# Entering the step loop of a graph kernel while the last sums before it still run

## The chip, the cores and the metric

The kernel runs on one core of a Trainium2 chip. The metric is the device time of one execution in microseconds (us): 748.04 us is the median of three runs of the kernel before (744.8 to 749.22). The engines are named as in the profile: PE is the matrix engine and PEld its weight load, DVE the vector engine, ACT the scalar engine, POOL the GpSimd engine. SP only issues transfers; ACT and POOL issue some too. Each engine works through its instructions in the order in which they were put on it, and an instruction that waits holds up those behind it.

## What is computed

Four graph layers over 2708 nodes with 128 features each; the adjacency `adj` is a 0/1 matrix. Each layer adds its result to x after a layer norm and a relu. The change lies in the last layer:

```
XW = X @ W                                  # 2708 x 128
s_col = XW @ a[:128];  s_row = XW @ a[128:]
den = exp(leaky_relu(s_row[:, None] + s_col[None, :], slope=0.01))
num = A @ den                               # 2708 x 2708, A is adj
att = where(num != 0, den / num, 0)
H   = A @ (att @ XW)
```

## The kernel before

The kernel doesn't compute num as a full matrix product. It ranks the nodes by s_row and cuts the ranking into chunks of `CH` = 124 nodes. For a column of den the leaky relu is on one branch for all nodes below a certain rank and on the other for all above it, so of num only the one chunk in which the branch changes needs a product over single nodes; all the others enter as prefix sums over whole chunks. The columns are put into 22 tables of 128 (`NE`), two chunks each, so there are 44 "slots" (`NS`).

The stage before the loop makes what the loop reads:

- `sums` (L1249): PE multiplies chunk weights `wts` with the transposed adjacency `adjt8`, kept in SBUF as fp8, 22 row tiles by 6 column blocks of 450 or 452 (`BLK`), into six PSUM accumulators. Row tiles 0 to 15 come for all blocks; the last `NTAIL` = 6 row tiles come pair by pair: blocks (0,3), (1,4), (2,5).
- For each pair (L1447 to L1470): DVE and ACT copy the accumulators to `s_sb`, PE turns them into prefix sums (L1456), ACT copies those to `flat` (L1462), DVE splits them into a high and a low half (`pre_hi` L1463, `pre_lo` L1464), and SP and ACT store these to `pre_d` in DRAM (L1468): 88 rows of 2708, four rows for each chunk.
- The table product (L1481): from `lanes_j` and `rhs_j` PE makes the table `jt`, from which DVE takes `c_two` (L1485 to L1492) and the indices `xw_i`. `c_two` is turned (L1501) and stored to `ctwo_d` (L1504).
- `first_densities` (L1550): DVE makes a diagonal of the first four slots' `c_two`, PE spreads it over all partitions with a product with `ones` (L1559), ACT makes the exponentials of both branches (`exponents`, L1530 and L1533), DVE their maximum and its two halves `d_hi`, `d_lo` (`densities`, L1542 to L1546).

What a slot q needs besides its densities is a tile `r` of 128 x 2708: rows 0 to 123 are adjacency rows, gathered by POOL as one byte each (`fetch`, L1512) and widened by DVE (`widen`, L1592, 124 x 2708); rows 124 to 127 are the four prefix rows of its chunk, loaded by SP from `pre_d` (`fetch_pre`, L1584), at an address that SP first reads from `pre_i` (`value_load`, L1583). Six tiles `r` and six `g` rotate.

The loop (L1630 on) has 22 steps s. Step s takes slots 2s and 2s+1 and makes, for each of six column blocks (`E0`, five of 512 and one of 148), four matmuls (L1646) and a logarithm on ACT (L1647); ACT then inverts (`invert`, L1619), DVE weighs (`weigh`, L1625), and two steps later PE adds the values into six accumulators (`spread_value`, L1600). Beside that each step makes the densities of two slots four ahead: SP loads their `c_two` values, spread over 128 partitions, from `ctwo_d` (`fetch_c`, L1570, 128 KB), and ACT makes the four exponentials after blocks 1 and 2. Every even step ACT issues a load of 1354 KB of the adjacency (`fetch_check`, L699), and every odd step DVE checks it (L695). After the last step the values go through one more product over all rows (after `lp.close()`); its rows come partly from tiles loaded during the last steps (`soon`, L1676).

The order on an engine comes from a planner, which lists instructions by the order in the text and by when it thinks their inputs are ready. Where `in_order()` or `pin` stands, an instruction is bound behind what was traced before it on its engine. In the kernel before, the stretch from L1438 to L1504 is left to the planner; the loop's matmuls, ACT and DVE work, gathers and row loads are pinned, `fetch_c` and `value_load` are not.

## Time and profile before

| what | us |
|---|---|
| median of three runs | 748.04 |
| the profiled execution, its own time | 749.01 |
| its span, first to last instruction | 747.1 |
| PE busy in the span | 656.5 (88%) |
| DVE busy | 583.3 (78%) |
| ACT busy | 468.7 (63%) |
| loop matmuls (L1646): first and last start | 450.1 and 664.8 |
| mean granted PE clock | 0.951 |

Positions in the profile are microseconds from the first instruction. The span is 1.9 us shorter than the profiled execution's own time, and that execution took 1.0 us more than the median. A row of the timeline gives start, duration, engine, line, operation, the tiles written and read, the shape and the count; in square brackets stands how long the engine had been idle before and what ended that. A row of busy time by stretch gives, for each engine, the busy time and in parentheses the number of instructions, and then the granted PE clock (1.00 is full speed), the mean busy share of the 16 DMA engines, and GB/s.

### The profile page before, as it was taken

Reading aid. Unit: us, or ns where it says so; the run is one execution under the profiler, and the core shown is the slowest. Engines: PE = TensorE matmul, PEld = TensorE weight load, DVE = VectorE, ACT = ScalarE, POOL = GpSimd, SP = SyncE. Lnnn points to the kernel's source line nnn. Section 1 sums busy time; section 2 is a strip of 40 time slices with the busy share of each in tenths; the row PEclk is TensorE's granted clock in tenths of the full one; section 3 lists DMA queues with packets and bytes.
Section 4 is the critical chain, followed back from the end, with each engine's and each line's share of the span. In section 5 each row is a group of like instructions: output and inputs, shape, how many; then the busy total and the mean of one; then the engine's idle time right before and its main releaser. Section 6 shows DMA issues by size and latency. Waiting matters only on the chain.

```text
span 747.1 us, 8635 instructions
## 1 busy us (share of the span) xinstructions
PE 656.5 (88%) x2775; PEld 421.5 (56%) x2775; DVE 583.3 (78%) x1019; ACT 468.7 (63%) x694; POOL 221.7 (30%) x198
## 2 busy tenths in 40 slices
PE   6889888978999999866998946999999999999994
PEld 3433333425678677634455614566666666657783
DVE  5999967968867885753798853999899899748972
ACT  5766667748856654425574533888888888765452
POOL 3320000141200210014570524366766766100000
PEclk9999998999999999986998986999999999999997
DMA  9699999765650799400100239857786776658711
GB/s 332 255 376 422 425 428 394 277 261 209 269 186 3 241 303 360 159 0 15 43 22 2 62 116 125 205 143 166 183 177 152 191 159 151 156 197 328 254 34 52
DMA packets 48679, 146.29 MB, mean 196 GB/s; under 512 B 12546, under 2 KB 27390, under 8 KB 40198
## 3 DMA queue, kind: packets, MB, share of 16 engines
q1 hardware_dynamic: 29288, 87.00, 34.6%
q10 hardware_dynamic: 4714, 34.74, 13.4%
...
## 4 chain that ended last, share of the span: by engine, by line
PE 50%; issue 15%; DVE 12%; ACT 7%; DMA 6%; POOL 3%; SPq 1%; ACTq 0%; POOLq 0%; DVEq 0%
PE bank L1646 14%; PE acc L1600 13%; PE acc L1763 5%; PE acc L614 5%; PE acc L1249 4%; DVE chk L695 3%; DMA chk<-in_adj_t_dram 2%; DVE m L483 2%; DMA adj_d<-a 2%; ACT adjt L216 2%; ACT y L474 1%; DMA c_row<-ctwo_d 1%; PE acc L1114 1%; POOL rstd L157 1%; PE bank L1012 1%
## 5 line engine op out<-in xcount | busy, mean ns | idle before, releaser
L1646 PE MATMUL bank<-r,d_hi 128*128 128x512 f32 (+1 forms) x264 | 142.3, 543 | 15.4 <-DMA r<-pre_d 9.7
L1600 PE MATMUL acc<-e,xw 128*128 128x512 f32 (+1 forms) x264 | 120.6, 544 | 0.0
L1647 ACT ACTIVATE ln<-bank,tiny 128x512 f32<-128x512 f32 x132 | 84.0, 636 | 48.7 <-PE bank L1646 43.2
L340 PE MATMUL acc<-tau,hw 128*128 128x512 f32 (+1 forms) x240 | 101.7, 572 | 12.9 <-DVE tau L348 12.9
L1512 POOL DMA_INDIRECT g<-adjt_d,row_i x44 | 90.5, 2057 | 37.5 <-DVE r L1592 14.3
L1646 PE MATMUL bank<-r,d_lo 128*128 128x512 f32 (+1 forms) x264 | 99.8, 382 | 0.0
L481 ACT CAST m<-a 128x660 fp32r<-128x660 fp8e4 (+1 forms) x45 | 55.2, 1233 | 53.1 <-PE acc L1763 30.7
L340 PEld LDWEIGHTS acc<-tau,hw 128*128 128x128 f32 x240 | 44.5, 197 | 71.9 <-issue 46.1
L1625 DVE SCALAR_TENSOR_TENSOR e<-row_b,sig,ln 128x1536 f32<-128x1536 f32 (+3 forms) x46 | 71.4, 1559 | 14.2 <-PE bank L1646 11.2
L348 DVE SCALAR_TENSOR_TENSOR tau<-row_b,sg,a 128x1536 f32<-128x1536 f32 (+1 forms) x44 | 70.8, 1623 | 11.1 <-DMA a<-in_adj_dram 10.1
L1646 PEld LDWEIGHTS bank<-r,d_hi 128*128 128x128 f32 x264 | 51.5, 195 | 48.9 <-issue 29.2
L695 DVE SCALAR_TENSOR_TENSOR chk<-chk 128x2708 f32<-128x2708 f32 (+1 forms) x22 | 65.4, 2975 | 10.2 <-DMA chk<-in_adj_t_dram 10.2
L1592 DVE CAST r<-g 124x2708 fp32r<-124x2708 fp8e4 x44 | 70.4, 1643 | 0.0
L371 ACT ACTIVATE a<-a 128x2708 fp8e4<-128x2708 f32 x22 | 54.1, 2458 | 24.7 <-issue 11.8
L1646 PEld LDWEIGHTS bank<-r,d_lo 128*128 128x128 f32 x264 | 51.6, 196 | 29.4 <-issue 24.0
L1619 ACT ACTIVATE ln<-ln 128x512 f32<-128x512 f32 (+2 forms) x68 | 62.8, 926 | 0.6 <-ACT ln L1647 0.6
L157 POOL TENSOR_TENSOR rstd<-isq,neg_half 128x4 f32<-128x4 f32 (+1 forms) x24 | 28.4, 1184 | 116.6 <-DVE isq L156 77.8
L1512 POOL DMA_INDIRECT xw<-xw_d,xw_i x22 | 41.6, 1892 | 62.5 <-PE acc L1600 52.2
L483 DVE CAST m<-a 128x2048 fp32r<-128x2048 fp8e4 (+1 forms) x43 | 39.5, 920 | 20.6 <-PE acc L614 11.1
L1600 PEld LDWEIGHTS acc<-e,xw 128*128 128x128 f32 x264 | 47.8, 189 | 12.2 <-issue 3.8
L614 PE MATMUL acc<-m,y_hi 128*128 128x512 f32 (+1 forms) x132 | 49.8, 384 | 5.4 <-DVE m L600 2.0
L614 PE MATMUL acc<-m,h_hi 128*128 128x512 f32 (+1 forms) x132 | 53.9, 416 | 0.1
...
## 6 DMA issues: line engine op xcount, KB each, us to landing
...
```

Of the source, the lines that this page charges most:

```text
L340: nc.tensor.matmul(accs[b][:, : hi - lo], stationary, tau[b // 3][:, o : o + hi - lo], start=first, stop=last)
L348: nc.vector.scalar_tensor_tensor(tau, row_b[:, h0:h1], sg[:, t : t + 1], tiles_a[t][:, h0:h1], ALU.max, ALU.mult)
L481: nc.scalar.copy(m[:, : hi - lo], src[:, lo:hi])
L614: nc.tensor.matmul(sums_of[phase, b][:, : hi - lo], part[:, t, :], tiles_m[k][:, lo - base : hi - base], start=t == 0 and i == 0, stop=t = ...
L695: lambda: nc.vector.scalar_tensor_tensor(a[:r], a[:r], 1.0, a[:r], ALU.is_equal, ALU.not_equal, accum_out=odd[:r, t : t + 1])
L1512: return nc.gpsimd.indirect_dma_start(out=out, out_offset=None, in_=src, in_offset=bass.IndirectOffsetOnAxis(ap=idx, axis=0),)
L1592: ins = nc.vector.tensor_copy(rows_r[q][:CH], g[:CH])
L1600: m = nc.tensor.matmul(ys_acc[b][:, : hi - lo], xws[s], waiting[s][:, lo:hi], start=(s == 0), stop=(s == NE - 1))
L1619: pin(nc.scalar.activation(lns[s][:, lo:hi], lns[s][:, lo:hi], AF.Exp, scale=-1.0))
L1625: nc.vector.scalar_tensor_tensor(waiting[s][:, lo:hi], row_b[:, lo:hi], sig[:, s : s + 1], lns[s][:, lo:hi], ALU.max, ALU.mult)
L1646: pin(nc.tensor.matmul(num[:, : hi - lo], d, a[:, lo:hi], start=(i == 0), stop=(i == 3)))
L1647: pin(nc.scalar.activation(lns[s][:, lo:hi], num[:, : hi - lo], AF.Ln, bias=tiny))
```

## The change

Only the stretch before the loop, the first step and the places of some tiles change; the same values are computed.

- The sums use the loop's column blocks `E0` instead of `BLK`.
- Each pair of column blocks gets a DRAM table of its own, `early_d[i]`. `store_pre(i)` stores a pair's prefix rows to it (two stores from SP, two from ACT), stores them to `pre_d` as well (four from SP), and loads the rows of slots 0 and 1 from `early_d[i]` into the pair's columns of `r` (four loads from SP).
- Slots 0 and 1 are gathered and widened before the sums end, into tiles of the pool `plan`, which is free by then; the gathers of slots 2 to 5 go to the pools `slot` and `steps`, which lie where `adjt8` lay. So six `g` tiles are two in `plan` and four in `slot`, and six `r` tiles are two of three tiles `wide3` in `plan` (the third is `ln` of the even steps) and four in `steps`.
- The whole stretch stands in `in_order()`. The table product comes right after the first pair's sums, the densities of slots 0 to 3 between the pairs; PE spreads `c_two` of slots 4 to 7 too (`cp4`), so that `fetch_c` begins with slot 8.
- Each `value_load` is bound behind the SP transfer traced before it (`chunk_of`).
- Step 0 takes its column blocks in the order 0, 3, 1, 4, 2, 5.
- Four tiles instead of six are loaded ahead for the last product (`soon`).

```diff
-
-    plan = ctx.enter_context(tc.tile_pool(name="plan", bufs=1, side="right", reuse_waits="tile"))
+    early_d = [dram.tile([4 * NC, 2 * 512], F32R, name=f"early_d{i}") for i in range(3)]
+
+    plan_stack = ExitStack()
+    plan = plan_stack.enter_context(tc.tile_pool(name="plan", bufs=1, side="right", reuse_waits="tile"))
...
-        bits = tabs.tile([P, N], BF16, tag="bits", name="bits", bufs=3)
+        bits = plan.tile([P, N], BF16, tag="wide3", name="bits", bufs=3)
...
-            junk = tabs.tile([P, N], BF16, tag="junk", name="junk", bufs=1)
+            junk = tab.tile([P, N], BF16, tag="far_off", name="junk")
...
         for b in blocks:
-            lo, hi = BLK[b]
+            lo, hi = E0[b]
...
-    pairs = [(b, b + 3) for b in range(3)]
...
+    def chunk_of(q):
+        traced = nc.cur_bb.bb.instructions
+        n = len(traced)
+        chunk_before = nc.sync.value_load(pre_i[0:1, q : q + 1], min_val=0, max_val=NC - 1)
+        load = traced[n]
+        issued = next(i for i in reversed(traced[:n]) if i.engine == load.engine and "DMA" in type(i).__name__)
+        tc.add_manual_dep(
+            load,
+            issued.name,
+            mybir.DependencyInfo(mybir.DependencyClass.NoSync, mybir.DependencyReason.DATA),
+            reason="chunk_of",
+        )
+        return chunk_before
+
+    def fetch_into(q, pool):
+        g = pool.tile([P, N], U8, tag="g8", name="g8", bufs=2 if pool is plan else 4)
+        pin(gather(g[:CH], adjt8_d[:, :], row_i[:CH, q : q + 1]))
+        rows8[q] = g
+
+    def widen(q):
+        g = rows8.pop(q).bitcast(F8)
+        pin(nc.vector.tensor_copy(rows_r[q][:CH], g[:CH]))
+
+    for q in range(2):
+        fetch_into(q, plan)
+    first_chunks = [chunk_of(q) for q in range(2)]
+    for q in range(2):
+        rows_r[q] = plan.tile([P, N], F32R, tag="wide3", name="r", bufs=3)
...
-    for i, pair in enumerate(pairs):
+
+    def evacuate(i):
+        for h, b in enumerate((i, i + 3)):
+            w = E0[b][1] - E0[b][0]
+            (nc.scalar.copy if h else nc.vector.tensor_copy)(s_sb[: 6 * NW, h, :w], SUMB[b][: 6 * NW, :w])
+
+    def last_sums(i):
         for t in range(T - NTAIL, T):
-            sums(t, pair)
+            sums(t, (i, i + 3))
+
...
-        lo, hi = BLK[i]
-        w = hi - lo
-        for h in range(2):
-            nc.scalar.copy(flat[64 * h : 64 * h + 2 * NC, lo:hi], p[64 * h : 64 * h + 2 * NC, :w])
-        ts_(pre_hi[:W108, lo:hi].bitcast(I32), flat[:W108, lo:hi].bitcast(I32), -4096, None, ALU.bitwise_and)
-        nc.vector.tensor_sub(pre_lo[:W108, lo:hi], flat[:W108, lo:hi], pre_hi[:W108, lo:hi])
-        for o, part_sb in ((0, pre_hi), (2 * NC, pre_lo)):
...
+        return p
+
+    def flatten(i, p):
+        for h, b in enumerate((i, i + 3)):
...
+    def store_pre(i):
+        pair = (i, i + 3)
+        ts_(pre_hi[:W108].bitcast(I32), flat[:W108].bitcast(I32), -4096, None, ALU.bitwise_and)
+        nc.vector.tensor_sub(pre_lo[:W108], flat[:W108], pre_hi[:W108])
+        parts = [(o, h, part_sb) for o, part_sb in ((0, pre_hi), (2 * NC, pre_lo)) for h in range(2)]
+        wide = [E0[b][1] - E0[b][0] for b in pair]
+        for o, h, part_sb in parts:
+            (nc.scalar if h else nc.sync).dma_start(
+                early_d[i][o : o + 2 * NC, h * 512 : h * 512 + wide[h]].bitcast(F32),
+                part_sb[64 * h : 64 * h + 2 * NC, : wide[h]],
+            )
+        for o, h, part_sb in parts:
+            lo, hi = E0[pair[h]]
+            nc.sync.dma_start(pre_d[o : o + 2 * NC, lo:hi].bitcast(F32), part_sb[64 * h : 64 * h + 2 * NC, : wide[h]])
+        early_rows = early_d[i].rearrange("(f c) n -> f (c n)", c=NC).bitcast(F32)
+        for q in range(2):
+            for h, b in enumerate(pair):
+                lo, hi = E0[b]
+                nc.sync.dma_start(
+                    rows_r[q][CH:, lo:hi].bitcast(F32),
+                    early_rows[:, bass.ds(first_chunks[q] * 1024 + h * 512, hi - lo)],
                 )
...
-    FIRST = 4
-    p = bank()
-    nc.tensor.transpose(p[:NS, :P], c_two_f, ident)
-    ctwo_t = row("ctwo_t", P)
...
+    diag = tab.tile([P, 8, P], F32, tag="far_off", name="diag")
...
+    def diagonal(s0):
...
+    def spread_c(s0):
+        p = acc_bank(0 if s0 == 0 else 3)
+        nc.tensor.matmul(p, ones, diag[:, s0 : s0 + 4].rearrange("p s q -> p (s q)"), start=True, stop=True)
+        return p
+
+    def first_exponents(s0, p):
...
+    def first_densities(s0):
...
+    with in_order():
+        last_sums(0)
+        evacuate(0)
+        jp = bank()
+        for t in range(T):
+            nc.tensor.matmul(jp[:, : 6 * NC], lanes_j[:, t, :], rhs_j[:, t, :], start=(t == 0), stop=(t == T - 1))
+        z4 = tab.tile([P, 4, P], F32, tag="lanes", name="z4")
+        low4 = tab.tile([P, 4, P], F32, tag="rhs", name="low4")
+        widen(0)
+        p0 = prefixes(0)
+        jt = row("jt", 6 * NC)
+        nc.vector.tensor_copy(jt, jp[:, : 6 * NC])
...
+        nc.vector.tensor_sub(c_two[:, :, 0], c_tab, gone)
+        nc.vector.scalar_tensor_tensor(c_two[:, :, 0], second, -3.0e4, c_two[:, :, 0], ALU.mult, ALU.add)
+        ts_(second, second, -1.0, 3.0e4, ALU.add, ALU.mult)
+        nc.vector.tensor_add(c_two[:, :, 1], gone, second)
+        diagonal(0)
+        flatten(0, p0)
+        store_pre(0)
+        last_sums(1)
+        p = bank()
+        nc.tensor.transpose(p[:NS, :P], c_two_f, ident)
+        cp = spread_c(0)
+        evacuate(1)
+        ctwo_t = row("ctwo_t", P)
+        nc.scalar.copy(ctwo_t[:NS], p[:NS, :P])
+        nc.sync.dma_start(ctwo_d.rearrange("(s q) -> s q", q=P), ctwo_t[:NS])
...
+        p1 = prefixes(1)
+        first_exponents(0, cp)
+        first_densities(0)
+        flatten(1, p1)
+        last_sums(2)
+        store_pre(1)
+        widen(1)
+        first_exponents(2, cp)
+        evacuate(2)
+        cp4 = spread_c(4)
+        first_densities(2)
+        p2 = prefixes(2)
+        nc.scalar.activation(sig, c_tab, AF.Exp, scale=0.99)
+        flatten(2, p2)
+        store_pre(2)
...
     def density_tiles():
-        z = steps.tile([P, 2, P], F32, tag="z", name="z", bufs=3)
+        z = steps.tile([P, 2, P], F32, tag="z", name="z", bufs=2)
...
-    def first_densities():
...
-            densities(s0, z, lower)
-
-    c_rows = {}
+    c_rows = {4: cp4[:, : 2 * P], 6: cp4[:, 2 * P :]}
 
     def fetch_c(s0):
         c_rows[s0] = p = steps.tile([P, 2 * P], F32, tag="c_row", name="c_row", bufs=3)
         nc.sync.dma_start(p, ctwo_d[s0 * P : (s0 + 2) * P].partition_broadcast(P))
...
     def fetch(q):
-        g = plan.tile([P, N], U8, tag="g8", name="g8", bufs=6)
-        pin(gather(g[:CH], adjt8_d[:, :], row_i[:CH, q : q + 1]))
-        rows8[q] = g
-
-    pre_rows = pre_d.rearrange("(f c) n -> f (c n)", c=NC).bitcast(F32)
+        fetch_into(q, plan if q % 6 < 2 else slot)
 
     def fetch_pre(q):
-        r = rows_r[q] = steps.tile([P, N], F32R, tag="r", name="r", bufs=6)
-        chunk_before = nc.sync.value_load(pre_i[0:1, q : q + 1], min_val=0, max_val=NC - 1)
+        if q % 6 < 2:
+            r = plan.tile([P, N], F32R, tag="wide3", name="r", bufs=3)
+        else:
+            r = steps.tile([P, N], F32R, tag="r", name="r", bufs=4)
+        rows_r[q] = r
+        chunk_before = chunk_of(q)
         pin(nc.sync.dma_start(r[CH:, :].bitcast(F32), pre_rows[:, bass.ds(chunk_before * N, N)]))
...
-    for q in range(6):
+    for q in range(2, 6):
         fetch(q)
-    for q in range(6):
+    for q in range(2, 6):
         fetch_pre(q)
     for s in range(2):
         fetch_xw(s)
-    first_densities()
-    for q in range(2):
-        widen(q)
-    for s in range(2):
-        fetch_c(FIRST + 2 * s)
     lns, soon = {}, {}
...
     for s in range(NE):
-        coming = FIRST + 2 * s
+        coming = 4 + 2 * s
         if coming + 4 < NS:
             fetch_c(coming + 4)
-        if coming < NS:
+        fresh = coming < NS
+        if fresh:
             z, lower = density_tiles()
         if s + 2 < NE:
             fetch_xw(s + 2)
         for q in (2 * s + 2, 2 * s + 3):
             if q < NS:
                 widen(q)
-        lns[s] = steps.tile([P, N], F32, tag="ln", name="ln", bufs=2)
-        for b, (lo, hi) in enumerate(E0):
+        if s % 2:
+            lns[s] = steps.tile([P, N], F32, tag="ln", name="ln", bufs=1)
+        else:
+            lns[s] = plan.tile([P, N], F32, tag="wide3", name="ln", bufs=3)
+        for i, b in enumerate((0, 3, 1, 4, 2, 5) if s == 0 else range(NB)):
+            lo, hi = E0[b]
             num = bank()
-            for i in range(4):
-                d, a = dense[2 * s + i // 2][i % 2], rows_r[2 * s + i // 2]
-                pin(nc.tensor.matmul(num[:, : hi - lo], d, a[:, lo:hi], start=(i == 0), stop=(i == 3)))
+            for j in range(4):
+                d, a = dense[2 * s + j // 2][j % 2], rows_r[2 * s + j // 2]
+                pin(nc.tensor.matmul(num[:, : hi - lo], d, a[:, lo:hi], start=(j == 0), stop=(j == 3)))
             pin(nc.scalar.activation(lns[s][:, lo:hi], num[:, : hi - lo], AF.Ln, bias=tiny))
...
-            if coming < NS and 1 <= b <= 2:
-                exponents(coming + b - 1, c_rows[coming], z, lower, b - 1)
...
+                if s % 2 == 0:
+                    pin(fetch_check(slot, "slot", nc.scalar))
...
-        if s >= NE - 3:
-            for t in range(2 * (s - NE + 3), 2 * (s - NE + 4)):
-                soon[t] = plan.tile([P, N], U8, tag="g8", name="a8", bufs=6)
+        if s >= NE - 2:
+            for t in range(2 * (s - NE + 2), 2 * (s - NE + 3)):
+                soon[t] = slot.tile([P, N], U8, tag="g8", name="a8", bufs=4)
                 pin(nc.scalar.dma_start(soon[t], adjt8_d[cols(t), :]))
...
     lp.close()
+    plan_stack.close()
...
     n_soon = len(soon)
     for t0 in range(n_soon, T, 4):
         n = min(4, TF - t0)
-        a8[t0] = fin.tile([P, 4, N], F8, name=f"a8_{t0}")
+        a8[t0] = fin.tile([P, min(4, T - t0), N], F8, name=f"a8_{t0}")
```

## The prediction

> **What bounds the kernel now.** I read the page for the whole, then busy time by stretch, then the timeline and the chain around the loop's start. Of the busy-time rows, cut at the places where the work changes character:
>
> ```profile
> 427.00:442.00 15.00, 10.48 (x57) 4.99 (x54) 6.13 (x20) 5.76 (x13) 4.94 (x5) 1.00 0.48 148
> 442.00:450.10 8.10, 0.00 (x0) 0.00 (x0) 7.27 (x10) 1.88 (x6) 3.61 (x2) 0.50 0.18 37
> 450.10:461.20 11.10, 6.44 (x17) 4.43 (x17) 1.26 (x1) 2.89 (x6) 6.72 (x5) 0.65 0.98 101
> 461.20:472.80 11.60, 9.98 (x33) 6.86 (x33) 9.01 (x11) 10.21 (x19) 3.79 (x2) 0.80 0.91 218
> 472.80:664.80 192.00, 192.00 (x718) 126.69 (x718) 170.23 (x152) 154.98 (x253) 105.48 (x49) 1.00 0.70 165
> ```
>
> From 472.8, where step 2 begins, PE is full without a gap for 20 steps of 9.6 us. What lies before doesn't reach that: for 8.1 us PE has nothing, then come steps 0 and 1, which take 22.7 us for 10 us of matmuls. So the change is worth what it moves the start of step 2, and nothing else; the 274.3 us behind it (747.1 - 472.8) stay, if the steps stay what they are. Why step 0 is late and long, from the timeline:
>
> ```profile
> 436.83 0.29 DVE L1483 COPY jt<-bank 128x132 f32<-128x132 f32 x1
> ...
> 445.04 6.31 DVE L1592 CAST r<-g 124x2708 fp32r<-124x2708 fp8e4 x4
> 446.56 2.54 SPq L1584 DMA_DIRECT2D r<-pre_d  x6
> ```
> ```profile
> 450.15 0.76 PE L1646 MATMUL bank<-r,d_hi 128*128 128x512 f32 x1 [9.21 <-DMA r<-pre_d]
> ...
> 459.69 0.49 ACT L1530 ACTIVATE z<-c_row,r_hi,slope_hi 128x128 f32<-128x128 f32 x1 [4.22 <-DMA c_row<-ctwo_d]
> ...
> 461.19 0.79 PE L1646 MATMUL bank<-r,d_hi 128*128 128x512 f32 x1 [4.11 <-ACT ln L1647]
> ```
>
> The table product comes last, so densities and widening stand behind it on DVE. The first rows come from DRAM only when all prefixes are stored: loaded at 446.56, used at 450.15. In step 0, ACT stands for 4.2 us before exponentials of `c_row`, whose load was issued at 449.15, behind six row loads; the logarithms behind it wait, and with them PE, for 4.1 us. Step 1 (464.05 to 472.77, 8.7 us) is ACT's: six logarithms, four exponentials and 2.9 us of inversions are some 8.2 us, and no `spread_value` fills PE yet.
>
> **The stretch before the loop, step by step.** All times are positions in this span. PE finishes the sums of row tiles 0 to 15 and of pair 0 at about 426.1, as now (46 matmuls take 9.00 us from 417.38). The blocks of 512 and 148 instead of 452 cost nothing: the columns are the same.
>
> DVE now carries a fixed order. Copy of pair 0 (0.63 us for 452 columns, 0.71 for 512) to 426.8; `widen(0)`, 1.57, to 428.4 (its gather, issued at 418.23, has landed at 426.6); from `jt` to `c_two` 2.2 (436.83 to 439.01) to 430.6; diagonal 0.71; high and low halves 0.40 + 0.62, here 1.15, to 432.4; copy of pair 1 and second diagonal to 433.8, three small operations to 434.1. Then it waits for ACT, which holds two store issues of 0.3, half of pair 1's copy (0.54), the copy of `ctwo_t` (0.26) and four exponentials at 0.36 apart: 435.1. Densities 1.15 (442.51 to 443.7), halves of pair 1 to 437.5, `widen(1)` to 439.1, copy of pair 2 to 439.8, densities, then halves of pair 2: copy to `flat` takes 1.05 us now, `flat` 0.9, the halves 1.2, so 443.1. ACT's last store issue ends at 443.8, and only then can it take the first logarithm. PE is through at 441.3 and can do blocks 0 and 3 at once: both slots are widened, their densities made, pair 0's rows loaded. So **the loop's first matmul moves from 450.1 to about 441.5**. That gain isn't the end's.
>
> What ends last after that is the third pair's way through DRAM. A `pre_d` store issued at 440.72 had all its parts down at 442.7 (2.0 us); one issued at 429.37, while gathers were in flight, at 435.3 (5.9 us). With the last early store issued at 443.5, the loads can go out between 445.5 and 449.4, four at 0.43 us. The first row load now takes 3.6 us from issue to use. Blocks 2 and 5 of step 0 thus start between 450.5 and 455; I take 451.5, nearer to the free case, since only four gathers are then in flight.
>
> Then step 1 needs the rows of slots 2 and 3, which SP asks for behind those loads. Each costs 0.57 for the address (now bound to this place; before, 44 of them ran on SP from 417.3 to 452.4 and held up its stores) and 0.43 for the issue: the second goes out at 449.5 to 453.4. In the train of six issued from 446.56, the second took 4.7 us to its use, the third and fourth landed 5.5 and 7.0 us after issue, the sixth 10. Bounds: 449.5 + 4.7 = 454.2 and 453.4 + 10 = 463.4. Slots 2 and 3 stand fifth and sixth in a train whose first four are a fifth of a row long, so I take the fourth's 7.0 from 451: **458**. Their gathers, moved from 421 to after the sums (437 on, as their tiles now lie where `adjt8` is), land 8.5 us after issue by the median, 447; behind gathers 4 and 5 and other transfers up to 20.8 (the longest), 458. So that is hidden behind the rows, and it's the next thing late if the rows come sooner.
>
> Step 1 then takes its 8.7 us again. PE has stood from about 446 to 451 and again before 458, and after the present gap the granted clock was 0.50 until 455.7, with the matmuls 0.42 instead of 0.23 us apart: 20 of them at the low clock are 8.4 us, just ACT's time. I add 1.0. **Step 2 starts at 467.7 instead of 472.8.** Sum: 467.7 + 274.3 = 742.0 span, + 1.9 to the execution's own time = 743.9, against 749.0; less the 1.0 by which the profiled execution stood above the median: **743.0 us**.
>
> [...] The clock gives the row above: 0.50 after 442. [...]
>
> [...] The row loads landed one behind another, some 1.9 us apart (449.7, 451.2, 453.0, 455.0). [...]
>
> **The other edits.** The eight extra stores and the early loads per pair are 12 SP issues at 0.3 to 0.43, 4 to 5 us of SP in each 5 us between pairs: just hidden, behind DVE's chain. The second spread is one product of 1.13 on an idle PE, and takes away two of 20 `c_row` loads. The three-tile ring of `r` and `ln` frees tiles in the order in which they are asked for: rows of slots 6k and 6k+1 go where those of three steps earlier were, so the loop's steps cost nothing more; if an `ln` held a row load up, one step (9.6 us) of slack would hide it. Tiles loaded ahead for the last product: four instead of six; the first big load, issued at 665.09, landed at 673, and tile 4 is cast at 679, so it is hidden. The adjacency check behind it (landed 687.2, read at 688.34) gets some 1.7 us more transfer ahead of it: at most 0.6.
>
> **Rivals.**
>
> 1. *The rows come freely.* The last early stores land in 2.0 us and slots 2 and 3 within 4.7: step 1 at 454.2, step 2 at 463: 738.3. For it: in 442 to 450 the DMA engines are 0.18 busy. Against: those were 8 us without gathers, and the change puts four gathers just there.
> 2. *The gain is eaten by the check's load.* In step 0 ACT issues 1354 KB after block 1, at about 448, before slots 2 and 3 are asked for. Row loads issued at 463.63, after the present check's at 459.75, landed at 473.6, 10 us later. Then rows at 462 to 464, step 1 as now at 464, step 2 at 472: 747.5. The loop would begin sooner and be no earlier at step 2, so the change doesn't do what it says.
> 3. *The slower side: `c_row` loads ahead of the row loads.* `fetch_c` isn't bound; the planner already puts a load for step 1 (461.93) ahead of row loads that stand before it in the text (463.63). Three `c_row` tiles are free now, and if SP issues them ahead of the third pair's loads, while gathers are in flight, they cost what the present three took: issued 449.15 to 450.03, landed 459.7 to 465.5, some 10 to 15 us. Third pair at 459, rows of slots 2 and 3 behind the check at 470, step 2 at 480: 756. It decides if they land after 452; before that they cost nothing.
>
> **Chances and range.** Forecast (740.6 to 746) 0.40; rival 1 0.28; rival 2 0.14; rival 3 and other slow cases 0.18. A measurement of this kernel tells some 1% (7.5 us) from no change: faster by over 1% 0.28, within 0.54, slower 0.18. The range takes in rival 1's bound, with 2 us for the clock that may not fall (736), and reaches to rival 3's near side: 736 to 755.
>
> **What would show it.** Right: first L1646 near 441.5, no `c_row` wait in step 0, a wait of PE on `r<-early_d` in step 0 and on `r<-pre_d` before step 1, step 2 near 468, and 9.6 us for each later step. Wrong: PE waiting for `g` or for a widening at step 1 (the moved gathers), steps over 9.6 us, a stretch of sums that ends after 426, or a wait after 665.

## The result, and the profile after

The changed kernel takes 752.45 us (median of 20 runs, 746.98 to 758.02), the kernel before 747.85 (20 runs beside them). The ratio is 1.0064, with a 95% interval of 1.004 to 1.0088: a little slower, where 743.0 was forecast. Its profiled execution has a span of 755.0 us (before: 747.1).

The busy time by stretch of the changed kernel, cut where the character of the work changes (columns as in the prediction: window, its length, then PE, PEld, DVE, ACT, POOL with their instructions, then granted clock, share of the DMA engines and GB/s):

```profile
421.00:435.30 14.30, 11.12 (x65) 5.39 (x64) 12.69 (x28) 7.08 (x18) 3.78 (x3) 1.00 0.33 103
435.30:446.00 10.70, 5.67 (x14) 4.07 (x14) 4.10 (x5) 2.91 (x7) 9.18 (x6) 0.67 0.64 191
446.00:468.00 22.00, 4.76 (x12) 2.75 (x11) 5.92 (x6) 4.52 (x8) 9.96 (x8) 0.50 0.92 150
468.00:479.50 11.50, 8.56 (x24) 6.12 (x24) 3.52 (x5) 6.66 (x12) 0.00 (x0) 0.63 0.64 84
479.50:671.50 192.00, 191.99 (x715) 126.44 (x715) 169.19 (x152) 154.63 (x252) 107.90 (x51) 1.00 0.65 158
```

The loop's first matmul now stands at 435.3 (before: 450.1), and step 2 begins at 479.5 (before: 472.8). The last row is as full as before: 20 steps at 9.64 us in place of 9.62, and from step 2 to the end 275.5 us in place of 274.4. What changed is the middle: step 0 begins 15 us earlier and lasts 33 us instead of 14, most of it at half the clock with PE busy 4.8 of 22 us, while the DMA engines are 92% busy.

Both profiles reach the loop at different times for a reason of their own (below), so I count from the first gather, at 413.4 here and 418.2 before. From there to step 2 it was 54.5 us; now it is 66.1. The timeline of the changed kernel shows the way of the third pair's prefixes (start, duration from the first to the last of a group, queue, line, operation, and in brackets the idle time before it and what ended it):

```profile
433.96 1.20 SPq L1527 DMA_DIRECT2D pre_d<-pre_lo  x2
...
435.29 0.53 PE L1736 MATMUL bank<-r,d_hi 128*128 128x512 f32 x1
...
439.31 1.62 SPq L1532 DMA_DIRECT2D r<-early_d  x4
...
440.12 0.43 DVE L1516 TENSOR_SCALAR pre_hi<-flat 108x512 int32<-108x512 int32 x1 [4.80 <-DMA pre_d<-pre_hi]
...
446.01 0.74 SPq L1527 DMA_DIRECT2D pre_d<-pre_lo  x2
...
447.05 0.37 ACTq L699 DMA_DIRECT2D chk<-in_adj_t_dram  x1
447.08 2.00 SPq L1532 DMA_DIRECT2D r<-early_d  x4
...
454.93 4.87 SPq L1679 DMA_DIRECT2D r<-pre_d  x4
```

SP has the second pair's stores out by 435.2, but the loads that wait for them only from 439.31; DVE can't write the third pair's halves before 440.12, since their one buffer is still being read by the second pair's stores; the third pair's last store is out by 446.8, has landed at 454.8, and the row loads of slots 2 to 5, which need it, are issued from 454.93. The chain of work that ended last shows how these hang together (start, duration, what; a DMA row lasts from issue to landing), and SP's waits from 432 to 447 (who waits for what: total, times, longest) show the queue's part:

```profile
433.34 6.70 DMA pre_d<-pre_hi
...
440.12 0.44 DVE pre_hi L1516
440.58 5.08 DMA early_d<-pre_hi
445.68 0.29 SPq L1527
446.01 0.35 SPq L1527
446.41 8.39 DMA pre_d<-pre_lo
...
456.26 14.89 DMA r<-pre_d
471.29 4.62 PE bank L1736 x10
```
```profile
SPq L1532 <- DMA early_d<-pre_lo: 3.9, 1, 3.9
SPq L1527 <- DMA early_d<-pre_hi: 1.7, 1, 1.7
SPq L1527 <- DMA r<-early_d: 1.2, 1, 1.2
```

Three stores land one after another on this chain, 20.2 us, and then slot 3's row load. The first landing is the one for which DVE waits before it writes the one buffer again, the third is that of a store whose rows the row loads do need. The middle one hands on no data: SP's `pre_d` store at 445.68 (L1527) doesn't read what ACT's early store of 440.58 writes. In this trace the transfers of SP and ACT count on eight semaphores in turn (101 to 108), and 209 of the 217, all but the first on each semaphore, go out only after a wait for the transfer before them on their own semaphore. Here ACT's store and the one of 445.68 both count on 105, which told of the landing at 445.66, 5.08 us after the issue. In the second profile the three landings are 6.48, 5.84 and 5.93 us, the row load 9.00, and SP's three waits 4.0, 2.2 and 1.6. In the kernel before, between 418 and 447 us, SP waits once, 0.4 us, and for DVE; for no landing. In the kernel before (its second profile) the points of the timeline above are these:

```profile
438.59 0.30 SPq L1468 DMA_DIRECT2D pre_d<-pre_lo  x1
...
444.52 2.54 SPq L1584 DMA_DIRECT2D r<-pre_d  x6
...
457.84 0.37 ACTq L699 DMA_DIRECT2D chk<-in_adj_t_dram  x1
```

The last store had gone out by 438.9 and six row loads follow, slot 2's (the third) 29.5 us after the first gather; in the changed kernel slot 2's, the first of the four, goes out after 41.5. The waits of the changed kernel between 430 and 480 (total, times, longest) say the same from PE's and ACT's side:

```profile
PE bank L1736 <- DMA r<-early_d: 13.1, 3, 5.8
PE bank L1736 <- DMA r<-pre_d: 11.3, 2, 9.2
...
ACT ln L1737 <- DVE pre_lo L1517: 6.3, 1, 6.3
```

### The profile page after: what moved, and what is told of

The parts are those of the page before. It is cut to its first block, busy times and chain, and to the rows that moved or that the text cites. A ratio compares the mean times of both kernels' runs of the same rounds, so it can differ in the third digit from the quotient of the medians.

```text
span 755.0 us, 8695 instructions
## 1 busy us (share of the span) xinstructions
PE 654.0 (87%) x2777; PEld 418.7 (55%) x2777; DVE 584.3 (77%) x1020; ACT 468.4 (62%) x694; POOL 221.8 (29%) x198
## 3 DMA queue, kind: packets, MB, share of 16 engines
q10 hardware_dynamic: 4426, 33.98, 13.1%
## 4 chain that ended last, share of the span: by engine, by line
PE 51%; issue 14%; DVE 12%; DMA 8%; ACT 6%; POOL 3%; SPq 0%; ACTq 0%; POOLq 0%; DVEq 0%
PE bank L1736 14%; PE acc L1690 13%; PE acc L1854 7%; PE acc L614 7%; PE acc L1251 3%; DVE m L483 2%; DMA adj_d<-a 2%; DVE chk L695 2%; DMA r<-pre_d 2%; ACT adjt L216 2%; ACT y L474 1%; PE acc L1116 1%; DMA pre_d<-pre_hi 1%; POOL rstd L157 1%; DMA pre_d<-pre_lo 1%
## 5 line engine op out<-in xcount | busy, mean ns | idle before, releaser
L1736 PE MATMUL bank<-r,d_hi 128*128 128x512 f32 (+1 forms) x264 | 143.9, 549 | 25.2 <-DMA r<-early_d 13.1
L340 PE MATMUL acc<-tau,hw 128*128 128x512 f32 (+1 forms) x240 | 100.0, 562 | 14.1 <-DVE tau L348 14.1
L1736 PE MATMUL bank<-r,d_lo 128*128 128x512 f32 (+1 forms) x264 | 102.0, 391 | 0.0
L1444 POOL DMA_INDIRECT g<-adjt_d,row_i x44 | 87.8, 1996 | 47.0 <-DMA pre_d<-pre_lo 14.5
L1710 DVE SCALAR_TENSOR_TENSOR e<-row_b,sig,ln 128x1536 f32<-128x1536 f32 (+3 forms) x46 | 71.5, 1559 | 36.6 <-ACT ln L1704 25.4
L481 ACT CAST m<-a 128x660 fp32r<-128x660 fp8e4 (+1 forms) x45 | 55.2, 1233 | 53.2 <-PE acc L1854 31.7
L1736 PEld LDWEIGHTS bank<-r,d_hi 128*128 128x128 f32 x264 | 52.3, 198 | 59.3 <-issue 37.1
L348 DVE SCALAR_TENSOR_TENSOR tau<-row_b,sg,a 128x1536 f32<-128x1536 f32 (+1 forms) x44 | 70.8, 1623 | 11.9 <-DMA a<-in_adj_dram 11.9
L1736 PEld LDWEIGHTS bank<-r,d_lo 128*128 128x128 f32 x264 | 52.5, 199 | 29.8 <-issue 24.0
L1444 POOL DMA_INDIRECT xw<-xw_d,xw_i x22 | 45.0, 2043 | 64.6 <-PE acc L1690 63.1
L157 POOL TENSOR_TENSOR rstd<-isq,neg_half 128x4 f32<-128x4 f32 (+1 forms) x24 | 28.8, 1202 | 116.4 <-DVE isq L156 77.8
L483 DVE CAST m<-a 128x2048 fp32r<-128x2048 fp8e4 (+1 forms) x43 | 39.4, 919 | 20.7 <-PE acc L614 11.2
L614 PE MATMUL acc<-m,h_hi 128*128 128x512 f32 (+1 forms) x132 | 53.7, 414 | 0.1
```

Of the source, the lines that this page charges most:

```text
L340: nc.tensor.matmul(accs[b][:, : hi - lo], stationary, tau[b // 3][:, o : o + hi - lo], start=first, stop=last)
L348: nc.vector.scalar_tensor_tensor(tau, row_b[:, h0:h1], sg[:, t : t + 1], tiles_a[t][:, h0:h1], ALU.max, ALU.mult)
L481: nc.scalar.copy(m[:, : hi - lo], src[:, lo:hi])
L614: nc.tensor.matmul(sums_of[phase, b][:, : hi - lo], part[:, t, :], tiles_m[k][:, lo - base : hi - base], start=t == 0 and i == 0, stop=t = ...
L1444: return nc.gpsimd.indirect_dma_start(out=out, out_offset=None, in_=src, in_offset=bass.IndirectOffsetOnAxis(ap=idx, axis=0),)
L1710: nc.vector.scalar_tensor_tensor(waiting[s][:, lo:hi], row_b[:, lo:hi], sig[:, s : s + 1], lns[s][:, lo:hi], ALU.max, ALU.mult)
```

## The experiments

The first theory was that three things of the transition make it late: the one buffer for the halves, the gathers of slots 2 to 5 among the second pair's stores, and the check's 1354 KB load ahead of the row loads. Its rival: the tables by pairs are too many transfers whatever stands beside them. This is how all runs came out; the columns are us from the first gather to the row load of slot 2, to step 1 and to step 2, us from step 2 to the end (all from the profile), and the ratio to the kernel before with its interval (from the times).

| run | slot 2's load | step 1 | step 2 | behind | ratio |
|---|---|---|---|---|---|
| before, first and second profile | 29.3, 29.5 | 45.8, 46.2 | 54.5, 54.9 | 274.4, 274.6 | 1 |
| changed kernel | 41.5 | 54.7 | 66.1 | 275.5 | 1.0064 (1.004 to 1.0088) |
| a_again: the same again | 39.6 | 47.6 | 58.0 | 275.6 | 1.0044 (1.0008 to 1.0079) |
| x_own: second buffer | 37.8 | 47.4 | 57.2 | 275.3 | 1.0063 (1.0042 to 1.0083) |
| x_g45: gathers 4, 5 later | 39.4 | 46.8 | 58.9 | 275.1 | 1.0043 (1.0019 to 1.0067) |
| x_ahead: chunk numbers early | 39.6 | 46.8 | 57.5 | 274.9 | 1.0058 (1.0033 to 1.0083) |
| x_noearly: no tables by pairs | 30.4 | 44.1 | 51.8 | 278.0 | 1.0056 (1.0029 to 1.0084) |
| x_late: check moved a step | 38.7 | 45.0 | 55.5 | 284.5 | 1.0128 (1.0099 to 1.0156) |
| x_late2: check in steps 9, 10 | 37.6 | 41.7 | 53.6 | 285.8 | 1.0119 (1.0064 to 1.0174) |
| x_skip: check left out | 38.1 | 41.8 | 53.7 | 275.3 | 1.0018 (0.9986 to 1.005) |
| x_sp: checks spread | 40.1 | 46.2 | 56.3 | 275.4 | 1.0043 (1.0009 to 1.0077) |
| x_ahsp: x_ahead + x_sp | 39.3 | 46.2 | 56.1 | 275.5 | 1.0055 (1.0029 to 1.0081) |
| x_all2: late2 + own + g45 | 37.8 | 42.2 | 56.4 | 287.6 | 1.0146 (1.0085 to 1.0208) |
| x_nol2: noearly + late2 | 30.5 | 45.6 | 53.3 | 285.5 | 1.0085 (1.0047 to 1.0123) |
| x_noahsp: noearly + ahsp | 29.2 | 43.9 | 51.6 | 277.0 | 1.0013 (0.9978 to 1.0047) |
| x_best: noearly + numbers early, check in step 2 | 29.5 | 44.5 | 52.3 | 280.1 | 1.0074 (1.0045 to 1.0102) |
| x_best2: noearly + numbers early, checks spread, 8 blocks | 29.5 | 44.2 | 51.9 | 278.5 | 1.002 (0.9989 to 1.0051) |
| b_skip: before without the check | 29.5 | 46.0 | 54.7 | 274.6 | 0.999 (0.9962 to 1.0018) |
| b_first: before, check first | 29.8 | 46.3 | 55.2 | 274.3 | 1.0014 (0.9982 to 1.0047) |

One profile is one execution. The table's profile columns repeat well where the code is the same up to there (before: 54.5 to 55.2 four times), less well with tables by pairs (58.0 and 66.1 in two executions of the same kernel). At best the ratios tell 0.3%, some 2 us, from nothing.

### The same kernels again

The changed kernel and the kernel before were each profiled a second time.

> The changed kernel itself, unaltered, for a second profile of it on the chip of the runs beside it. Theory A (check's load, gathers and stores collide in every execution): first gather to step 2 again 62-67 us, steps 2 to 4 in 19.3. Theory B (the 66.1 of the first profile was one slow execution): under 60. Ratio to the kernel before 1.004-1.009 either way.

> The kernel before, unaltered, for a second profile of it. All sums so far stand on one profile of it (first gather at 418.2, 54.5 to step 2, 274.3 behind). Theory A: it lost 2-3 us ahead of the first gather in that profile by chance, since five profiles of kernels with the change have it at 414.0-416.4 and their code is the same up to the sums; then first gather at 415-417, 54-55.5 to step 2, span 743-746. Theory B: the change itself brings the first gather forward: 418 or later again.

The changed kernel's second profile has 58.0 where its first had 66.1; A had asked for 62 to 67 and B for under 60, so B: the first profile overstates the loss, but a loss stays. In the first, row loads issued at 454.93 were used 13 us later; in the second, issued at 460.59, 8 us later. The check's load had gone out 7.9 us ahead of them in the first (447.05) and 0.5 us ahead in the second (460.12). The kernel before gave 54.9 (54.5), and its first gather stood at 416.0 instead of 418.2: A there. The place of the first gather varies: counted from the end of the layer before (its last sum), it came after 89.6 to 92.1 us in four profiles of kernels without the change and 87.7 to 93.0 in sixteen with it. In the rank stage, at the start of this stretch, the granted clock stays at 0.50 for 20.5 and 17.1 us in the two profiles of the kernel before and for 10.2 and 23.9 in the two of the changed kernel, and the first gather comes after 92.1, 89.6, 87.9 and 93.0: the longer at 0.50, the later in these four. The means are 91.1 and 89.2; whether the change has part in these 1.9 us isn't settled.

### One delay at a time: buffer, gathers, chunk numbers

```diff
+    pre_hi1 = merge.tile([P, 512], F32, name="pre_hi1")
+    pre_lo1 = plan.tile([P, 512], F32, tag="first2", name="pre_lo1")
+    halves_of = [(pre_hi, pre_lo), (pre_hi1, pre_lo1), (pre_hi, pre_lo)]
...
+        pre_hi, pre_lo = halves_of[i]
```

> The second pair's halves get buffers of their own, so that the third pair's (in the first pair's buffers again) needn't wait until the second pair's stores have landed; all else as in the changed kernel. Theory A (the one pair of buffers is the first link that comes late): the 4.8 us wait on a DMA before the third pair's upper halves and the 6.3 us of the loop's first logarithm go, the third pair's loads are issued some 4-5 us earlier, and first gather to step 2 falls from 66.1 to 61-63, median 748-750. Theory B (the DMA engines are full there; the buffer's wait only shows it): the wait moves to the landings behind it, first gather to step 2 stays within 1.5 of 66.1, median 751-753.

```diff
-    for q in range(2, 6):
+    for q in range(2, 4):
         fetch(q)
...
-        for q in (2 * s + 6, 2 * s + 7):
+        for q in (4, 5, 6, 7) if s == 0 else (2 * s + 6, 2 * s + 7):
             if q < NS:
                 fetch(q)
```

> The gathers of slots 4 and 5 are issued behind step 0 instead of together with those of slots 2 and 3 ahead of it; all else as in the changed kernel. Theory A (four gathers in the same stretch as the second pair's stores hold those up): the second pair's stores, landed up to 438.8, land 2-3 us earlier, and with them the third pair's halves; first gather to step 2 falls to 62-64.5, median 748.5-750.5. Theory B (the gathers fill bandwidth that nobody waits for): within 1.5 of 66.1, median 751-753.

```diff
-    first_chunks = [chunk_of(q) for q in range(2)]
+    first_chunks = [chunk_of(q) for q in range(8)]
...
-        chunk_before = chunk_of(q)
+        chunk_before = first_chunks[q] if q < len(first_chunks) else chunk_of(q)
```

> The chunk numbers of the first eight slots are all read into SP's registers ahead of the first pair's stores, where the changed kernel reads two there and every other one in its place, between two row loads; all else as in the changed kernel. In the profiles SP issues the row loads of slots 2 to 5 at 1.3-1.4 us each in the changed kernel and at 0.45 in the kernel before. Theory A (the reads in place delay the rows): issues 0.45-0.5 apart again, the rows of slot 3 0.9 us and those of slots 4 and 5 1.8-2.7 us earlier, first gather to step 2 1-2.5 us shorter than the 58-66 of the changed kernel, ratio 1.001-1.004. Theory B (the rows are late by their landing, not by their issue): issues closer, landings as before, ratio 1.004-1.007.

None of the three brought more than 1 us beside the second profile of the changed kernel (58.0), and their ratios can't be told from its own. That is B's side in all three, though the theories of the first two were counted from 66.1, and by the letter 57.2 and 58.9 lie below both. (Expectations written later quote 58.2 and 59.9 for the first two; those were read at step 2's first `spread_value`, 1 us behind its first matmul.) The buffer is the instructive one. With its second buffer DVE writes the third pair's halves 4.1 us earlier, and yet SP's first store of them goes out 29.3 us after the first gather (27.6 and 27.4 in the changed kernel), the last at 31.3 (33.0 and 33.6). The timeline of that kernel:

```profile
437.01 7.55 SPq L1536 DMA_DIRECT2D r<-early_d  x4
...
437.76 0.43 DVE L1520 TENSOR_SCALAR pre_hi<-flat 108x512 int32<-108x512 int32 x1 [1.03 <-DMA pre_d<-pre_lo]
...
444.67 0.31 SPq L1525 DMA_DIRECT2D early_d<-pre_hi  x1
...
446.23 0.81 SPq L1531 DMA_DIRECT2D pre_d<-pre_lo  x2
...
453.13 4.36 SPq L1683 DMA_DIRECT2D r<-pre_d  x4
```

The halves are ready at 438.9. But the four loads of the second pair's rows stand ahead of the third pair's stores in SP's queue. Three of them are out by 438.2; the fourth goes out at 444.31, and the first store of the third pair behind it at 444.67. What the fourth load waits for is a landing, as SP's waits and the chain of that kernel say:

```profile
SPq L1536 <- DMA early_d<-pre_hi: 5.9, 1, 5.9
```
```profile
438.22 6.07 DMA early_d<-pre_hi
444.31 0.25 SPq L1536
```

The store of 438.22 is ACT's first one of the third pair. The load reads nothing of it; by the trace's releaser it waits on the semaphore on which that store counts, 5.9 us. So the buffer's wait is gone, and the queue holds the stores up all the same. In the changed kernel the same four loads waited 3.9 us (4.0 in its second profile) for stores of the second pair that they do read. In both the late stores come from the queue: a load that waits for a landing, put ahead of the next pair's stores. (The loads behind the stores of the next pair, with the tables kept, weren't tried, nor were more semaphores.)

The chunk numbers are a cost of their own, but a hidden one. In the changed kernel SP reads each number from SBUF between two row loads; the issue times of its second profile:

```profile
460.59 4.32 SPq L1679 DMA_DIRECT2D r<-pre_d  x4
...
466.32 1.65 SPq L1679 DMA_DIRECT2D r<-pre_d  x2
```

and with eight numbers read ahead:

```profile
455.94 1.71 SPq L1679 DMA_DIRECT2D r<-pre_d  x4
...
458.30 0.75 SPq L1679 DMA_DIRECT2D r<-pre_d  x2
```

Four row loads in 1.71 us instead of 4.32, and step 2 no more than 0.5 us sooner: it isn't the issues that it waits for.

### The tables by pairs

```diff
-        for o, h, part_sb in parts:
-            (nc.scalar if h else nc.sync).dma_start(
-                early_d[i][o : o + 2 * NC, h * 512 : h * 512 + wide[h]].bitcast(F32), ...
         for o, h, part_sb in parts:
-            nc.sync.dma_start(pre_d[o : o + 2 * NC, lo:hi]...
+            (nc.scalar if h else nc.sync).dma_start(pre_d[o : o + 2 * NC, lo:hi]...
-        early_rows = ...          # and the four loads from it
...
         store_pre(2)
+        for q in range(2):
+            nc.sync.dma_start(rows_r[q][CH:, :].bitcast(F32), pre_rows[:, bass.ds(first_chunks[q] * N, N)])
...
-        for i, b in enumerate((0, 3, 1, 4, 2, 5) if s == 0 else range(NB)):
+        for i, b in enumerate(range(NB)):
```

> The tables by pairs are left out: per pair only the four stores to the common table are issued, and the rows of slots 0 and 1 are loaded whole from it once the third pair is stored, as the rows of the other slots are; the early table product, the early gathers, the second spread from TensorE and the loads of the check stay as in the changed kernel. Theory A (the early tables cost more in transfers than the early start is worth): the loop's first matmul moves from 435.3 back to 444-449, but first gather to step 2 falls to 56-60 (54.5 in the kernel before, which issues the same transfers), median 743-747. Theory B (the early start of step 0 pays, and the loss is the check's load and the buffers alone): first gather to step 2 is 66 or more, median 752 or more.

A's direction, and further than its 56 to 60: 51.8 from the first gather to step 2. The loop begins at 34.5 us instead of 21.9, and step 2 is 6.2 to 14.3 us earlier. Its timeline:

```profile
437.73 0.29 SPq L1521 DMA_DIRECT2D pre_d<-pre_lo  x1
...
442.72 0.76 SPq L1615 DMA_DIRECT2D r<-pre_d  x2
...
444.54 4.35 SPq L1669 DMA_DIRECT2D r<-pre_d  x4
```

The last store goes out at 437.73 and five microseconds later all have landed: the row loads follow at 442.72, 28.6 us after the first gather, as in the kernel before, although the sums end 2.1 us later (the table product now stands among them) and the third pair's halves begin 4.1 us later. In all eleven profiles with tables by pairs slot 2's load went out at 37.6 to 41.5 us, in all nine without them at 29.2 to 30.5. That is the step where the change loses what it gains: the early rows start a step 0 that then waits, and the stores and loads that bring them hold up the rows of slots 2 and 3, which step 1 needs.

The time didn't follow: 1.0056. From step 2 to step 4 it took 22.3 us in place of 19.3, and the stretch behind step 2 is 278.0. DVE waits there for the check's load, step 1 now being earlier than the load:

```profile
DVE chk L695 <- DMA chk<-in_adj_t_dram: 5.4, 1, 5.4
```

That takes back what step 2 had gained (2.7 to 3.1 us) and 0.3 to 0.9 more; it doesn't explain all of the 4 us that 1.0056 stands for. The profiled execution was the fastest of its five (745.78, median 748.48).

### The check's load

In the changed kernel ACT issues it at 447.05, ahead of the last early loads (at 460.12 in the second profile, just ahead of the row loads). Three kernels put it elsewhere, two leave it out, one puts it first in the kernel before.

```diff
# x_late: load in step 1, comparison in step 2
-                if s % 2 and s < NE - 1:
+                if s > 1 and s % 2 and s < NE - 1:
...
+            if s == 1 and i == 1:
+                pin(fetch_check(slot, "slot", nc.scalar))
+            if s == 2 and i == 1:
+                pin(check())
# x_late2: none in steps 0 and 1, one more in steps 9 and 10
+                if s in (3, 5, 7, 9, 10, 11, 13, 15, 17, 19):
                     pin(check())
+                if s in (2, 4, 6, 8, 9, 10, 12, 14, 16, 18, 20):
                     pin(fetch_check(slot, "slot", nc.scalar))
# x_sp: loads at these blocks of the loop, comparison six blocks behind
+    LOADS = (14, 25, 36, 47, 57, 68, 79, 90, 101, 111, 122)
+            if 6 * s + i - 6 in LOADS[:-1]:
+                pin(check())
+            if 6 * s + i in LOADS:
+                pin(fetch_check(slot, "slot", nc.scalar))
```

> The loop's first check is moved one step on: its 1354 KB load is issued in step 1 instead of step 0, and the check itself runs in step 2; all else as in the changed kernel. The times of step 2's first matmul in the profile (479.5 us in the changed kernel, 472.8 in the kernel before) is the yardstick, counted from the first gather (66.1 and 54.5). Theory A (the check's load lies in the DMA engines ahead of the third pair's rows and of the last stores to the common table): the rows of slots 2 and 3, landed at 467.9 and 471.2, land by 461-463, step 1 begins at 461-463 instead of 468.05, first gather to step 2 falls to 58-61, median 745-748. [...]

> The first check of the loop is left out of steps 0 and 1: loads are issued in steps 2, 4, 6 and so on, and one more load and check stand in steps 9 and 10, so that the same number of checks is made, none of them less than a step after its load; all else as in the changed kernel. In the run in which the load was only moved into step 1 and its check early into step 2, first gather to step 2 fell to 55.4, but VectorE then waited 4.4 us for the load in step 2 and steps 2 to 4 took 28.6 in place of 19.3. Theory A (the check's load in the transition is most of the loss): first gather to step 2 54-57, steps 2 to 4 19-20, ratio 0.993-0.999. Theory B (the load only takes the place of others that are late too): steps 2 to 4 again 23 or more, ratio 1.003 or more.

> The loop's eleven check loads are spread over steps 2 to 20, one every ten or eleven blocks instead of every twelve, beginning in step 2 instead of step 0; each check stands six blocks behind its load as before; all else as in the changed kernel. In the run that left steps 0 and 1 free of the check but put two checks into steps 9 and 10, first gather to step 2 took 53.6 (66.1 and 58.1 in two profiles of the changed kernel) and steps 9 to 12 took 38.9 in place of 28.9. Theory A (the check's load in steps 0 and 1 is the larger part of the loss): first gather to step 2 53-56, 9.6-9.7 for each step behind it, ratio 0.993-0.999. Theory B (every microsecond given to the transition is paid again by VectorE in the loop, which is busy 19 of 20 us there): steps of 9.8 or more, ratio 1.003 or more.

Up to step 2 all three went theory A's way: 55.5, 53.6 and 56.3 in place of 58.0. By the ratios none did, and two of the kernels were the slowest of all but one. The waits in step 2 of the first:

```profile
ACT ln L1737 <- DVE z L1653: 8.2, 1, 8.2
DVE chk L695 <- DMA chk<-in_adj_t_dram: 4.4, 1, 4.4
```

DVE reaches the comparison 4.4 us before the load has landed, the densities stand behind it, and ACT's logarithms behind those for 8.2 us: from step 2 to step 4 it took 28.5 us instead of 19.3. In the second, the double check of steps 9 and 10 cost 10 us (38.9 from step 9 to step 12 in place of 28.9). There ACT waits, between 536 and 578:

```profile
ACT ln L1737 <- DVE chk L695: 9.1, 2, 4.6
```

The load is an instruction in ACT's queue, it needs the buffer that the comparison frees, and where both stand in one step, the logarithms stand behind both. The third kernel has neither fault, keeps its steps at 9.64, and comes to 1.0043, which can't be told from the changed kernel.

> The changed kernel with the loop's first check left out altogether, its 1354 KB load and VectorE's 3 us instruction: one of 21 tiles isn't compared, so the time is that of a kernel with less work. It bounds what any other place for it could give. Theory A (the load among the third pair's transfers costs 4-8 us): first gather to step 2 54-57, steps 9.6, ratio 0.996-1.001, with 1.004-1.006 of the changed kernel beside it. Theory B (with the load gone, the tables by pairs keep step 2 late): first gather to step 2 58 or more, ratio 1.002 or more.

> The kernel before with the loop's first check left out in the same way (its load and its comparison, one of 21 tiles). Theory A (here the load is issued 11 us behind the first row loads and costs little): first gather to step 2 53.5-54.5, ratio 0.998-1.001. Theory B (it costs as much here as in the changed kernel): ratio 0.994 or less.

> The kernel before, with only this changed: the load of the loop's first check is issued by ScalarE ahead of the row loads (about 440 us, behind the third pair's stores) instead of in step 0 (457.8 us, 11 us behind them). The comparison stays in step 1. If the place of this load is what costs in the changed kernel, where it is issued at 447.05 and the row loads from 454.9, then it must cost here too. Theory A: the rows land 4-10 us later, first gather to step 2 58-64 (54.5 and 54.9 in two profiles of the kernel before), ratio 1.004-1.010. Theory B (the load only fills engines that stand idle): 54-56, ratio 0.998-1.002.

```diff
# x_skip, b_skip: the first check's tile isn't compared
-                if s % 2 and s < NE - 1:
+                if s > 1 and s % 2 and s < NE - 1:
...
+                if s == 0:
+                    unchecked.pop(0)
...
# b_first: before the row loads
+    pin(fetch_check(slot, "slot", nc.scalar))
     for q in range(6):
         fetch_pre(q)
...
-            if b == 2 and s % 2 == 0:
+            if b == 2 and s and s % 2 == 0:
```

Without the load and its comparison the changed kernel's step 2 comes after 53.7 us and its ratio is 1.0018: A by the profile; the ratio lies between A and B and its interval takes in both. Leaving it out of the kernel before changes nothing (0.999). And issued ahead of the row loads in the kernel before, it costs nothing either, against my theory A (58 to 64):

```profile
442.74 0.37 ACTq L699 DMA_DIRECT2D chk<-in_adj_t_dram  x1
...
443.92 0.30 SPq L1468 DMA_DIRECT2D pre_d<-pre_lo  x1
...
450.22 2.54 SPq L1584 DMA_DIRECT2D r<-pre_d  x6
```

The check's load goes out 7.5 us ahead of the row loads; the loop's first matmul stands at 453.7, 3.5 us behind the first row load, as in the second profile without it (444.52 and 448.0). But this isn't the place that the load has in the changed kernel, for by the time of the row loads it has landed:

```profile
442.80:449.30 6.50, 2.08 (x2) 0.50 (x2) 2.47 (x8) 3.03 (x9) 2.22 (x3) 0.50 0.79 272
449.30:450.20 0.90, 0.00 (x0) 0.00 (x0) 0.90 (x1) 0.00 (x0) 0.00 (x0) 0.50 0.03 8
450.20:453.70 3.50, 0.00 (x0) 0.02 (x1) 3.50 (x4) 0.00 (x0) 2.75 (x1) 0.50 0.23 37
```

Up to 449.3 the DMA engines are 0.79 busy, then 0.03, and beside the first row load 0.23, as in the profile without it. What the load does hold up is the last two stores, which land 6.1 us after their issue in place of 1.7 to 2.0; SP reads chunk numbers meanwhile and then waits only 0.6 us for them. So this run doesn't show what the load does to row loads beside which it is under way.

The table does, with one execution for each kernel. With tables by pairs and the load ahead of the row loads (five profiles) step 1 comes 7.2 to 13.1 us after slot 2's load went out, and most, 13.1, where the check's load was longest under way before it; with the load moved or left out (six) it is 3.7 to 6.9. Step 2 comes at 57.2 to 66.1 with it (step 1 at 46.8 to 54.7), at 53.6 to 56.4 without (41.7 to 46.2). Without the tables (b_first apart) ACT comes to the load only at 40.3 to 41.9 us, when slots 2 and 3 have their rows, and it makes no difference up to step 2 (51.8 and 52.3 with it, 51.6, 51.9 and 53.3 without). So tables and load do harm together: the tables bring the row loads so late that the check's load is under way beside them. How much is the load's isn't sharp: x_late2 and x_sp, which run the same instructions up to step 2, reach step 1 at 41.7 and 46.2. And how much of the time it is, the ratios don't tell: 0.9986 to 1.005 without it.

### Together

> The changed kernel with three things at once: the check moved as in the second run, buffers of their own for the second pair's halves, and the gathers of slots 4 and 5 behind step 0. Alone the buffers gave first gather to step 2 of 58.2 and the gathers 59.9, against 66.1 of the changed kernel. Theory A (they are links of one chain, store landings to row loads, and add up in part): 48-53, ratio 0.988-0.994. Theory B (each takes away the same wait): 54-57, within 0.002 of the run with the check moved alone.

> No tables by pairs (rows of slots 0 and 1 whole from the common table after the third pair) and the first check moved as in the run beside it. With the tables by pairs gone alone, first gather to step 2 was 51.8 and steps 2 to 4 took 22.4, VectorE waiting 5.4 us for the check's load. Theory A (check's load and tables by pairs are two separate losses): first gather to step 2 50-52, steps 2 to 4 19-20, ratio 0.990-0.996, below that of the run with the check moved alone by 0.003 or more. Theory B (once the check is out of the way, the early start of step 0 pays): ratio above that of the run beside it.

> Both edits of the two runs before it: check loads from step 2 on, and eight chunk numbers read ahead. Theory A (two separate delays): first gather to step 2 51-54, ratio 0.991-0.996, 0.001-0.003 under the run with the check loads alone. Theory B (one hides the other): within 0.001 of that run.

> As the run before it, and without the tables by pairs: the rows of slots 0 and 1 are loaded whole from the common table behind the third pair's stores. Theory A (the early start of step 0 is worth nothing, since step 1 waits for the third pair's way through the common table in both): first gather to step 2 49-52, ratio 0.988-0.994, under the run with the tables. Theory B (the early start pays once nothing else is late): ratio above that run's by 0.002 or more.

The first two carry the 10 to 12 us of the double check in steps 9 and 10. The first is B by its step 2 (56.4), the second (53.3 and 1.0085) neither. In the first, step 1 begins at 42.2 but lasts 14.2 us (11.9 in x_late2): PE stood 4.8 us in it for slot 3's rows instead of 2.8. Gathers 4 and 5 are now issued beside the row loads, at 452 to 454; that they hold the rows up wasn't shown by itself. Chunk numbers and check together (1.0055) are worth nothing that can be told: B. Without the tables as well, 1.0013 (interval 0.9978 to 1.0047): A by its place below the run with the tables, though far above A's 0.988 to 0.994. The two intervals overlap, so this isn't shown. Step 2 came at 51.6, 3 us sooner than in the kernel before, and the stretch behind it gave 2.4 back, 1.9 of it in steps 11 to 14, where DVE waited 5.3 us for a load issued six blocks earlier.

> The changed kernel without the tables by pairs, with eight chunk numbers read ahead, and with the first check compared in step 2 instead of step 1 (its load stays in step 0, where ScalarE comes to it behind the row loads); nothing is left out of the computation. Without the tables alone, steps 2 to 4 took 22.4, VectorE waiting 5.4 us for that load in step 1. Theory A (what is left of the change is a gain of the second spread and of the early table product): first gather to step 2 50-52.5, steps 2 to 4 19.3, ratio 0.993-0.998. Theory B (the profiles of these kernels so far were their faster runs): ratio 0.999-1.003.

> No tables by pairs, eight chunk numbers read ahead, and the eleven check loads spread from step 2 to 20 with each comparison eight blocks behind its load (six in the run without tables that came to 1.0013, where VectorE waited 5.3 us for one load in step 12 and steps 12, 13 and 15 together took 1.7 us too long). Nothing is left out of the computation. Theory A (what is left of the change is a gain of 2-3 us): first gather to step 2 51-52.5, 9.6-9.7 for each step, ratio 0.994-0.999. Theory B (it is worth nothing by itself): ratio 0.999-1.003.

Both were meant to keep those 3 us, and neither beats the kernel before (1.0074, and 1.002 with 0.9989 to 1.0051). In the first, comparison and next load stood in one step again (ACT waited 4.8 us; 24.0 from step 2 to step 4). In the second, the comparison eight blocks behind its load fell ahead of the densities in steps 9 and 18, and each took 11.1 us. Which place for the check keeps the gain, or whether there is one, stays open.

## Why the prediction was wrong, step by step

All in us from the first gather (the forecast's at 418.2); first and second profile of the changed kernel.

| step of the prediction | forecast | measured |
|---|---|---|
| loop's first matmul | 23.3 | 21.9, 21.9 |
| third pair's last early store issued | 25.3 | 28.8, 28.5 |
| first of its loads issued | 27.3 to 31.2 | 33.7, 34.3 |
| blocks 2 and 5 | 32.3 to 36.8, took 33.3 | 36.5 and 44.5; 37.4 and 40.3 |
| slot 3's rows asked for | 31.3 to 35.2 | 42.9, 40.9 |
| step 1 | 36.0 to 45.2, took 39.8 | 54.7, 47.6 |
| step 1 lasts | 9.7 | 11.5, 10.4 |
| step 2 | 49.5 | 66.1, 58.0 |
| from there to the end | 274.3 | 275.5, 275.6 |

- **Right:** what bounds the kernel (step 2's start sets the end), the order of DVE and ACT up to step 0, that the early start isn't the end's, and roughly the size of step 1 (10.4 and 11.5 instead of 9.7; PE waits 1.2 and 2.1 us in it for slot 3's rows, and its clock was 0.63 in the first profile). The signs named for being right came, PE waiting in step 0 for `r<-early_d` and before step 1 for `r<-pre_d` and no `c_row` wait, only with other sizes. Rival 3 didn't come: `fetch_c` went out behind the row loads (459.84, after four of them).
- **The step that failed** is the sentence that the eight extra stores and the early loads are "just hidden, behind DVE's chain". I added up SP's issues, 4 to 5 us for each pair, and put its waits at nothing. SP waits 3.9, 1.2 and 1.7 us for landings between the second pair's loads and the third pair's last store (4.0, 1.6 and 2.2 in the second profile), where the kernel before waits for none. The first is the early loads' wait for the stores that they read, with the next pair's stores behind them; the other two are stores that wait because their semaphore is still taken by an early store and an early load. In x_own, with a second buffer, it is 5.9 us on one early load. Beside that I overlooked that `pre_hi` and `pre_lo` are one buffer for three pairs where the kernel before had columns of its own for each; DVE's halves of the third pair came 4.1 to 4.3 us later for it. On the chain that ended last these are two more landings (6.70 and 5.08 us; 6.48 and 5.84) ahead of the one that the forecast had. And I let slots 2 and 3 be asked for right behind the early loads, though they need the last `pre_d` store, which the change puts behind the early ones; the row load that waits for it went out after 41.5 and 39.6 us, where 31.3 to 35.2 was the forecast even for the next one.
- **The landing of stores** was taken at 2.0 to 5.9 us; the last `pre_d` store took 8.4 and 5.9.
- **The rows' way** was taken at 7.0 us from the issue of slot 3's load to its use; it was 9.0 in the second profile and 15.0 in the first, beyond the bound of 10. (By the trace's semaphores the third and fourth load of the train before landed 6.0 and 7.6 us after issue, where I had read 5.5 and 7.0.)
- **Address reads:** 0.57 for each was right in kind (1.3 to 1.4 us from one row load to the next, 0.45 with the numbers read ahead), and worth nothing, since landing was the limit.
- **Rival 2** (the check's load eats the gain, 747.5) named the right shape, a loop that begins sooner and a step 2 that doesn't. Its price, 10 us for a row load behind the check's load, is near what was measured where the two are under way together: 7.2 to 13.1 us to the first use, against 3.7 to 6.9 without it. What it had not is when slot 2's row load goes out (41.5 and 39.6), where 31.3 to 35.2 was the forecast for slot 3's. By the forecast's own sum rivals 2 and 3 come to 747.2 and 755.2 instead of 747.5 and 756; nothing rests on that.
- **Gathers 2 to 5 "hidden behind the rows":** held in both profiles of the changed kernel: PE never waited for a gather or a widening before step 2. Issuing two of them later gained nothing; in that run PE did wait for a widening, 3.3 us before step 1.
- **The tail** was taken at 0.6 at most; from the last loop matmul to the end it is 82.8 and 83.0 us in place of 82.1 and 82.3.

The times agree with the profiles in size. The second profiles of both kernels differ by 3.1 us up to step 2 and 1.0 behind it, the first ones by 11.6 and 1.1, and the median by 4.6. The range 736 to 755 held the time, and 0.6% lies within the 1% that had 0.54, but by luck: the upper end came from rival 3's `c_row` loads, which didn't come, and the forecast had the sign wrong.
